# Decoder layer: the first two tiles become the first and second halves of two sequences

## The chip, the cores and the metric

The kernel runs on one core of a Trainium2 chip, in one launch. Its metric is the device time in microseconds (us), the median of several runs. Engines: PE is TensorE, DVE VectorE, ACT ScalarE, POOL GpSimd, SP the engine whose queue starts most DMAs. PEld is TensorE's loading of weights.

## What is computed

Sixteen sequences of 128 tokens with 256 features go through one decoder layer, in float32:

```python
scores = einsum('bhqd,bhkd->bhqk', q, k) / sqrt(16)       # 16 heads, q, k, v from x
scores = where(causal, -inf, scores)
vals, idx = top_k(scores, 32)                             # only the 32 largest keys of a query count
attn = softmax(scores at idx, -inf elsewhere)
x = layernorm(x + (attn @ v) @ Wo.T + bo)
o = relu(x @ proj_in[e].T) @ proj_out[e].T                # for each of 8 experts e
x = layernorm(x + sum over e of gate[e] * o)              # gate[e]: sum of a token's weights whose id is e
xq = quantize(x @ H, 4 bits);  x = layernorm(x + xq @ ternary(weight).T)
```

## The kernel before, in words

The sequences are cut into tiles of 1, 1, 2, 2, 2, 2, 2, 2, 2 sequences (SIZES, line 35). A tile's attention is done in units: one unit is eight heads (one of two halves c of the features) of one sequence, so 32 units. A query of a block of 32 queries sees at most 32, 64, 96 or 128 keys; BLOCKS lists the eight blocks of a unit (two groups of four heads by four query blocks), PLACE their columns in a row of 640 scores.

For each unit: `queries_keys` (264) projects q and k for a feature half of a tile and lays q out in block-diagonal form in `qblk` (for later tiles with eight small DMAs, for the first with multiplications by a mask), `attn_scores` (327) makes four score matmuls, copies them to SBUF on ACT and adds the causal mask on POOL; unit 0 gets its mask by two bf16 matmuls instead. `attn_weights` (357) is the top-k on DVE: four rounds of MAX8 (the eight largest) and MATCH_REPLACE8 (marks them as taken), on blocks with more than 32 keys; blocks with 32 keys take one MAX8 for the softmax's maximum. ACT makes the exponentials. `attn_finish` (405) sums, keeps the taken keys and divides; the division is mostly on POOL. `attn_turn` (421) transposes the weights on PE into `pta` and `ptb` and ACT copies them to `pT`; `attn_apply` (439) multiplies by the values. `attn_end` (450) ends a tile: `py` is the output projection, then residual and norm on DVE, and the transposed result `x1T` (466, through `px`) is what the experts read. `experts` (507) makes for each of eight experts two double halves `ph` (line 551), their relu on ACT, and `po` (521), which ACT scales with the gate and POOL adds up. `token_gates` (481) makes the gates, `ffn` (624) is the last part, run piecewise among the next tile's experts.

The order on PE, DVE, ACT and POOL is that in which the program writes the instructions. A unit has nine steps (STEPS); `plan` says at which step of the running unit other work is written: scores of the next unit at step 1, projections six units ahead, `values` and `residual` (`carry`), the turn of a unit, the end of a tile. `pace` spreads the experts of tile t evenly over the steps between `begin[t]` and `begin[t + 1]`. LAG sets `attn_finish` one step later for units that are not the last of a tile. SP's queue holds the loads, the `qblk` DMAs and the experts' weights (1 MB each), which are written after the projections of (tile 2, half 0) and (tile 3, half 0); the weights of experts 0 to 2 come with the first, of 3 to 7 with the second. Buffers: `xT`, `x`, gate inputs three deep, so a fourth tile's x waits for the first tile's last read of its own.

Of the kernel before, what the change touches and what calls it, by code (L numbers as in the profile page):

```python
# [17 lines left out]
P = 128  # L18
# [11 lines left out]
def decoder_kernel(ctx: ExitStack, tc: tile.TileContext, i: dict, out: bass.AP):  # L30
# [3 lines left out]
    E, DFF = 8, 512  # L34
    SIZES = (1, 1, 2, 2, 2, 2, 2, 2, 2)
    FIRST = [sum(SIZES[:t]) for t in range(len(SIZES))]
# [4 lines left out]
    FIRST_UNITS = DC * SIZES[0]  # L41
# [38 lines left out]

    def load_x(t):
        x = b3.tile([P, TB, D], F32, tag="x", name=f"x{t}")
        nc.sync.dma_start(x[:, : SIZES[t]], i["x"][tokens(t), :].rearrange("(b p) d -> p b d", p=P))
        return x
# [4 lines left out]
    def load_gates(t):  # L89
        n, bs = SIZES[t], slice(FIRST[t], FIRST[t] + SIZES[t])  # L90
        w = b3.tile([P, TB, S], F32, tag="ctx", name=f"ctx{t}")
        nc.sync.dma_start(w[:, :n], i["ctx_512"][bs].rearrange("b k s -> k b s"))
        k = b3.tile([P, TB, S], I32, tag="tok", name=f"tok{t}")
        nc.sync.dma_start(k[:, :n], i["itok"][bs].rearrange("b k s -> k b s"))
        return w, k
# [10 lines left out]
    xT0 = load_T(0, nc.sync)  # L106
# [7 lines left out]
    loaded = xT0, load_x(0)  # L114
    for w, name in ((wqT, "WqT"), (wkT, "WkT")):
        nc.sync.dma_start(w[:, :, ts(1, P)], i[name].rearrange("(c p) o -> p c o", p=P)[:, :, ts(1, P)])
    wvT = weight("WvT", [(nc.sync, slice(0, D))])
    next_loaded = load(1, nc.sync)
# [66 lines left out]
    mask16 = [b1.tile([P, TB, D], BF16, tag=tag, name=f"mask_{tag}").rearrange("p b d -> p (b d)") for tag in ("qi", "qiT")]  # L185
    nc.vector.memset(mask16[0], 0.0)
    nc.vector.memset(mask16[1][:, :P], 0.0)
    for z in (kTs[0], kTs[1], qblks[0][:, 1], odd(vms[0])):
        nc.vector.memset(z, 0.0)
    nc.vector.tensor_reduce(cmask, cm4.rearrange("p h k -> p k h"), AX.X, ALU.add)  # L190

    for k, at, step, count, width in ((0, 320, 128, 2, 2), (0, 96, 128, 2, 1), (1, 32, 64, 2, 1)):
        nc.gpsimd.tensor_copy(
            view(mask16[k], at, [[step, count], [32, width], [1, 32]]),
            cmask.unsqueeze(1).unsqueeze(1).to_broadcast([P, count, width, 32]),
        )
    nc.vector.memset(pTs[0], 0.0)
    for kT in kTs[2:4]:
        nc.gpsimd.memset(kT, 0.0)
    for z in (odd(vms[1]), qblks[1], qblks[2], qblks[3], kTs[4]):  # L200
        nc.gpsimd.memset(z, 0.0)
# [10 lines left out]
    PLACE = {(0, 3): 0, (1, 3): 128, (0, 2): 256, (0, 0): 352, (1, 2): 384, (1, 0): 480, (0, 1): 512, (1, 1): 576}  # L212
    BLOCKS = [(0, 0), (1, 0), (0, 1), (1, 1), (0, 2), (1, 2), (0, 3), (1, 3)]

    def keys(m):
        g, j = BLOCKS[m]
        return slice(PLACE[g, j], PLACE[g, j] + 32 * (j + 1))

# [45 lines left out]
    def queries_keys(t, c, xT):  # L264
# [5 lines left out]
        for j, w in enumerate((wqT, wkT)):  # L270
            for cc in range(DC):
                nc.tensor.matmul(  # L272
                    pps[j][:, j, : n * S], w[:, cc, ts(c, P)], xT[:, cc, : n * S], start=cc == 0, stop=cc == DC - 1
                )
        kT = kTs[(t * DC + c) % len(kTs)]
        qblk = qblks[t] if n == 1 else qblks[(t * DC + c + 2) % len(qblks)]
        if n == 1:
            qblk = qblk[:, c : c + 1]
        ins = None
        if (t, c) == (0, 0):  # L280
            for h in range(HG):
                nc.vector.tensor_scalar(
                    qblk[:, 0, :, h], pps[0][:, 0, :S].rearrange("p (m q) -> p m q", q=32),
                    bq[:, c : c + 1], hmask[:, h : h + 1], ALU.add, ALU.mult,
                )
        else:
            qT = b2.tile([P, TB, S], F32, tag="qT", name=f"qT{t}_{c}")
            ins = nc.scalar.activation(
                qT[:, :n], pps[0][:, 0, : n * S].rearrange("p (b s) -> p b s", b=n), AF.Identity, bias=bq[:, c : c + 1]
            )  # L290
        for g in range(2):
            rows = ts(g, 64)
            ins = nc.scalar.activation(
                kT[rows, :n, g], pps[1][rows, 1, : n * S].rearrange("p (b s) -> p b s", b=n), AF.Identity,
                bias=bk[rows, c : c + 1],
            )
        if (t, c) == (0, 1):
            for h in range(HG):
                src = qT[:, 0].rearrange("p (m q) -> p m q", q=32)
                if h % 2:  # L300
                    nc.scalar.activation(qblk[:, 0, :, h], src, AF.Copy, scale=hmask[:, h : h + 1])  # L301
                else:
                    ins = nc.gpsimd.tensor_scalar(qblk[:, 0, :, h], src, hmask[:, h : h + 1], None, ALU.mult)  # L303
        elif (t, c) != (0, 0):
            for h in range(HC):
                ins = nc.sync.dma_start(
                    qblk[ts(h, DH), :n, :, h % HG].rearrange("p b m q -> p (b m) q"),
                    qT[ts(h, DH), :n].rearrange("p b (m q) -> p (b m) q", q=32),
# [3 lines left out]
    def values(t, xT, x):  # L312
        for b in range(SIZES[t]):
# [13 lines left out]
    def attn_scores(n, qblk, kT, b):  # L327

        parts = [psum(f"ps{k}_{n}") for k in range(2)]
        if n == 0:  # L330

            for k, cols in enumerate((slice(0, 512), slice(512, ROW))):
                part = parts[k][:, : cols.stop - cols.start]
                nc.tensor.matmul(part, ident16, mask16[k][:, : cols.stop - cols.start], start=True, stop=False)
        for j in (3, 2, 1, 0):
# [3 lines left out]
                qblk[:, b, j].rearrange("p h q -> p (h q)"), kT[:, b, :, : 32 * (j + 1)], start=n > 0, stop=n > 0 or j < 2,  # L339
            )  # L340
        if n == 0:

            return lambda m: parts[keys(m).start // 512][:, keys(m).start % 512 :][:, : keys(m).stop - keys(m).start], ins
        sc = b2.tile([P, ROW], F32, tag="sc", name=f"sc{n}")
# [8 lines left out]
        return lambda m: sc[:, keys(m)], ins  # L353
# [3 lines left out]
    def attn_weights(n, sc):  # L357
# [3 lines left out]
        weights[n] = wk  # L361

        nc.gpsimd.memset(wk[:, keys(1)], 0.0)  # L363
        m8 = b2.tile([P, len(BLOCKS), TOPK], F32, tag="m8", name=f"m8{n}")
        nb = b2.tile([P, len(BLOCKS)], F32, tag="nb", name=f"nb{n}")
        z = b2.tile([P, len(BLOCKS)], F32, tag="z", name=f"z{n}")
        d8 = b2.tile([P, len(BLOCKS) - 2, TOPK], F32, tag="d8", name=f"d8{n}")

        def exponentials(ms):

            for m in ms:
                nc.scalar.activation(  # L372
                    ex[:, keys(m)], sc(m), AF.Exp, bias=nb[:, m : m + 1], scale=SCALE,
                    accum_out=z[:, m : m + 1] if m < 2 else None,
# [3 lines left out]
        for r in range(TOPK // 8):  # L378
            left = (lambda m: wk[:, keys(m)]) if r else sc
            for m in range(0 if r == 0 else 2, len(BLOCKS)):  # L380
                nc.vector.max(m8[:, m, ts(r, 8)], left(m))  # L381
            if r == 0:
                nc.vector.tensor_scalar(nb, m8[:, :, 0], -SCALE, None, ALU.mult)
            if r == TOPK // 8 - 1:

                (nc.gpsimd if 3 < n <= LAST[2] else nc.vector).tensor_tensor(
                    d8, m8[:, 2:], m8[:, 2:, 0:1].to_broadcast([P, len(BLOCKS) - 2, TOPK]), ALU.subtract
# [3 lines left out]
            if r == 1 + late:  # L391
                exponentials(range(4))
            if r == 2:
                exponentials(range(4, len(BLOCKS)))
            for m in range(2, len(BLOCKS)):
                nc.vector.match_replace(wk[:, keys(m)], m8[:, m, ts(r, 8)], left(m), TAKEN)  # L396
            yield
        unfinished[n] = wk, ex, z, d8
# [6 lines left out]
    def attn_finish(n):  # L405

        wk, ex, z, d8 = unfinished.pop(n)
        nc.vector.tensor_reduce(z[:, 2:], d8, AX.X, ALU.add)
        rz = b2.tile([P, len(BLOCKS)], F32, tag="rz", name=f"rz{n}")
        nc.vector.reciprocal(rz, z)  # L410
        for cols in (slice(0, PLACE[0, 0]), slice(PLACE[1, 2], ROW)):
# [532 lines left out]
```

## Time and profile before

| | |
|---|---|
| median of 3 runs | 644.65 us (643.78 to 645.05) |
| the profiled execution | 642.72 us, its span 641.0 us |
| busy share of the span | PE 95%, PEld 81%, DVE 78%, ACT 54%, POOL 47% |
| granted TensorE clock, mean | 0.985 |
| experts: ph (line 551) and po (521) | 240.8 and 238.4 us of PE |
| replaces (396) and maxima (381), all forms | MATCH_REPLACE8 132.1 + 42.7, MAX8 100.4 + 38.3 us of DVE |
| first experts' matmul of tiles 0, 1, 2 | 46.49, 88.73, 137.5 us |
| first maxima (start) of the units 0 to 7 on DVE | 8.77, 20.97, 33.54, 50.96, 63.38, 78.42, 92.23, 103.14 us |
| weights of experts 0 and 1 issued on SP | 31.90 to 33.60 us |

A slice of the busy rows is a fortieth of the span, each digit tenths. In a row of the trace, "x8" counts instructions, the mean is in ns, and what stands behind "idle before" or "<-" is what ended the engine's wait. Instructions overlap a little, so a group's time from start to start is shorter than its busy time.

### The profile page before, as it was taken

The page shows a single profiled execution, that of the slowest core. Times are in us where ns is not written, and L with a number is a line of the kernel's source. Part 1 is how long each engine was busy: PE and PEld are TensorE (multiplying, and loading weights), DVE is VectorE, ACT ScalarE, POOL GpSimd, SP SyncE. Part 2 cuts the span into 40 slices and gives each one's busy share as a digit, 9 for nine tenths or more (in the row PEclk, how much of TensorE's full clock was granted, in tenths as well). Part 3 has the DMA queues.
Part 4 walks back from the last instruction along what each step waited for, and adds up shares of the span by engine and source line. Part 5 has one row for each costly group of instructions (what it writes and reads, how often), then busy time and mean ns, then how long its engine had stood idle before and what let it go on. Part 6 is the DMA issues. An engine that isn't in the chain of part 4 may idle for free.

```text
span 641.0 us, 12490 instructions
## 1 busy us (share of the span) xinstructions
PE 605.9 (95%) x3534; PEld 521.9 (81%) x3534; DVE 503.1 (78%) x3133; ACT 346.5 (54%) x1030; POOL 303.5 (47%) x574
## 2 busy tenths in 40 slices
PE   6579999989999999999999999999999999999993
PEld 5468888878888888888888888888888888888882
DVE  7989799799956995789957898579978997332256
ACT  4746666755556565546655655655555655432121
POOL 7114455423753367424772457434673458324322
PEclk9969999999999999999999999999999999999997
DMA  6176700010001000010000000000000000000000
GB/s 205 17 222 214 235 3 10 18 41 2 10 18 38 21 4 16 8 42 2 10 17 19 25 1 10 1 25 2 1 2 0 18 2 2 1 21 0 1 2 33
DMA packets 37990, 21.13 MB, mean 33 GB/s; under 512 B 19104, under 2 KB 35872, under 8 KB 37920
## 3 DMA queue, kind: packets, MB, share of 16 engines
q1 hardware_dynamic: 37360, 20.20, 10.8%
q8 instruction: 28, 0.46, 0.3%
q14 instruction: 42, 0.34, 0.2%
q10 hardware_dynamic: 560, 0.13, 0.1%
HBM read 16.26 MB, written 2.10 MB: 29 GB/s over the span
## 4 chain that ended last, share of the span: by engine, by line
PE 77%; DVE 11%; ACT 5%; POOL 2%; issue 2%; DMA 1%; SPq 1%; ACTq 0%; DVEq 0%; POOLq 0%
PE ph L551 30%; PE po L521 29%; PE ps L337 4%; PE pqk L272 3%; DVE wk L396 3%; PE ptb L445 2%; PE py L457 2%; PE pta L427 2%; DVE m L381 2%; POOL wk L416 2%; PE pv L316 1%; DVE junk L500 1%; ACT ex L372 1%; DVE wk L412 1%; ACT pT L437 1%
## 5 line engine op out<-in xcount | busy, mean ns | idle before, releaser
L551 PE MATMUL ph<-x1T,w_in 128*128 128x256 f32 (+1 forms) x1152 | 240.8, 358 | 0.7 <-ACT hT L555 0.6
L521 PE MATMUL po<-w_out,hT 128*128 128x256 f32 x1024 | 238.4, 381 | 0.0
L551 PEld LDWEIGHTS ph<-x1T,w_in 128*128 128x128 f32 x1152 | 198.7, 190 | 26.5 <-issue 3.4
L521 PEld LDWEIGHTS po<-w_out,hT 128*128 128x128 f32 x1024 | 189.6, 190 | 24.5 <-issue 1.4
L555 ACT ACTIVATE hT<-ph 128x512 f32<-128x512 f32 (+1 forms) x144 | 78.9, 549 | 133.7 <-PE ph L551 133.2
L396 DVE MATCH_REPLACE8 wk<-m,wk 128x64 f32<-128x64 f32 (+2 forms) x576 | 132.1, 239 | 0.0
L529 ACT ACTIVATE part<-po,gate 128x256 f32<-128x256 f32 x112 | 52.9, 472 | 93.2 <-PE po L521 92.5
L381 DVE MAX8 m<-wk 128x8 f32<-128x64 f32 (+2 forms) x576 | 100.4, 241 | 0.0
L416 POOL TENSOR_TENSOR wk<-wk,rz 128x128 f32<-128x128 f32 (+2 forms) x92 | 47.4, 540 | 92.9 <-DVE wk L412 92.9
L532 POOL TENSOR_TENSOR acc<-acc,part 128x512 f32<-128x512 f32 (+1 forms) x56 | 64.4, 1149 | 46.5 <-ACT part L529 45.8
L372 ACT ACTIVATE ex<-sc,nb 128x32 f32<-128x32 f32 (+1 forms) x248 | 74.2, 350 | 0.0
L636 POOL TENSOR_TENSOR xh<-xh 128x256 f32<-128x256 f32 x98 | 67.6, 711 | 1.2
L352 POOL TENSOR_TENSOR sc<-sc,cmask 128x64 f32<-128x64 f32 (+1 forms) x93 | 32.2, 373 | 56.7 <-ACT sc L346 56.7
L337 PEld LDWEIGHTS ps<-kT,qblk 128*128 128x128 f32 x256 | 41.1, 192 | 5.4 <-POOL qblk L303 1.4
L396 DVE MATCH_VALUE_LOAD wk<-m,wk 128x8 f32 x576 | 44.5, 77 | 0.0
L337 PE MATMUL ps<-kT,qblk 128*128 128x256 f32 (+3 forms) x256 | 42.9, 311 | 1.3 <-ACT qblk L301 1.0
L500 DVE SCALAR_TENSOR_TENSOR junk<-wt 128x128 f32<-128x128 f32 x128 | 43.2, 365 | 0.2
L396 DVE MATCH_REPLACE8 wk<-m,sc 128x64 f32<-128x64 f32 (+1 forms) x186 | 42.7, 241 | 0.0
L437 ACT COPY pT<-pta 96x256 f32<-96x256 f32 (+2 forms) x96 | 35.2, 366 | 6.9 <-PE pta L427 6.1
L381 DVE MAX8 m<-sc 128x8 f32<-128x32 f32 (+1 forms) x248 | 38.3, 225 | 0.0
L639 DVE TENSOR_REDUCE qs<-xh 128x2 f32<-128x512 f32 x7 | 4.8, 685 | 36.0 <-POOL xh L636 36.0
L427 PE MATMUL pta<-ident,wk 128*128 128x128 f32 x128 | 20.2, 281 | 12.6 <-POOL wk L363 8.9
(177 smaller groups left out, 667.0 us busy)
## 6 DMA issues: line engine op xcount, KB each, us to landing
w_in<-in_w_in SPq DMA_DIRECT2D x8, 512.0 KB, 6.2
w_out<-in_w_out SPq DMA_DIRECT2D x8, 512.0 KB, 7.1
xT<-in_xT SPq DMA_DIRECT2D x7, 256.0 KB, 3.6
x<-in_x SPq DMA_DIRECT2D x7, 256.0 KB, 2.7
qblk<-qT SPq DMA_DIRECT2D x112, 16.0 KB, 1.9
out_y<-y SPq DMA_DIRECT2D x7, 256.0 KB, 2.1
ctx<-in_ctx SPq DMA_DIRECT2D x7, 128.0 KB, 2.2
tok<-in_itok SPq DMA_DIRECT2D x7, 128.0 KB, 2.2
```

Source lines behind the costliest of these rows:

```text
L337: ins = nc.tensor.matmul(view(parts[PLACE[0, j] // 512], at, [[step, 2], [1, 32 * (j + 1)]]), qblk[:, b, j].rearrange("p h q -> p (h q)"), ...
L372: nc.scalar.activation(ex[:, keys(m)], sc(m), AF.Exp, bias=nb[:, m : m + 1], scale=SCALE, accum_out=z[:, m : m + 1] if m < 2 else None,)
L381: nc.vector.max(m8[:, m, ts(r, 8)], left(m))
L396: nc.vector.match_replace(wk[:, keys(m)], m8[:, m, ts(r, 8)], left(m), TAKEN)
L416: eng.tensor_tensor(view(wk, at, [[step, 2], [1, size]]), view(src, at, [[step, 2], [1, size]]), rz[:, 2 * j : 2 * j + 2].unsqueeze(2).to_ ...
L500: nc.vector.scalar_tensor_tensor(junk, wt[:, 1, b], float(e), wt[:, 0, b], ALU.is_equal, ALU.mult, accum_out=gate[:, b, e : e + 1],)
L521: nc.tensor.matmul(po, hT[:, f, ts(b, S)], w_out[:, e, f], start=f == 0, stop=f == FC - 1)
L529: nc.scalar.activation(part[:, b], po, AF.Copy, scale=gates[t][:, b, e : e + 1])
L532: sums.append(lambda: nc.gpsimd.tensor_tensor(acc[:, :n], (acc if e else x1)[:, :n], part[:, :n], ALU.add))
L551: nc.tensor.matmul(ph[:, f, : n * S], w_in[:, e, c, ts(2 * k + f, P)], x1T[:, c, : n * S], start=c == 0, stop=c == DC - 1,)
L555: ins = nc.scalar.activation(hT[:, ts(k, 2), : n * S], ph[:, :, : n * S], AF.Relu)
L636: nc.gpsimd.tensor_tensor(pairs(xh, c, half), pairs(from_, 0, half), pairs(from_, 1, half), op)
```

## The change

The first two tiles no longer hold one sequence each. Tile 0 is the first 64 tokens of sequences 0 and 1, tile 1 their last 64 tokens; both still have 128 tokens. A query in tile 0 sees at most 64 keys. Units (SUBS, 34 in all):

- tile 0: two EARLY units, each eight heads of both first halves, four blocks of 64 keys with top-k and four of 32 keys. The score is not copied: it stays in PSUM, with its mask by a bf16 matmul of 384 columns.
- tile 1: four LATE units, each eight heads of one sequence's second half, two blocks of 96 and two of 128 keys.

Tile 0 now needs the values of both sequences (made together), and one `xT` buffer, `kT` and `qblk` are shared by the halves. `xT` and `x` of the first two tiles are loaded in more, smaller DMAs, and tile 1's result is stored in two. The projections (1, 0), (1, 1), (2, 0), (2, 1) move to steps 3, 12, 21 and 30; before, (1, 0), (1, 1), (2, 0), (2, 1), (3, 0) stood at 3, 5, 7, 12 and 21. Tile 2's values move from step 7 to 23, tile 3's into the general plan. Experts' weights 0 to 2 now follow projection (1, 1), 3 to 7 follow (2, 0). The subtraction for d moves from POOL to DVE in tile 2's four units, the preparation of the last weights from steps 38 to 56 to 60 to 78, and `begin[1]` from 14 to 10 steps after its last unit.

```diff
+    SUBS = (1, 2, 2, 2, 2, 2, 2, 2, 2)
+    HALF = S // 2
...
+    def load_half(xT, t):
+
+        src = i["xT"][:, : 2 * S].rearrange("(c p) (b h s) -> h c p b s", p=P, b=2, h=2)
+        for c in range(DC):
+            nc.sync.dma_start(view(xT[:, c], t * HALF, [[S, 2], [1, HALF]]), src[t, c])
...
+    EARLY = [(2 * P + 32 * k, 32) for k in range(4)] + [(HALF * k, HALF) for k in range(4)], 4, [(0, 2 * P)], [(4, 4), (0, 4)]
+    LATE = [(256, 96), (352, 96), (0, P), (P, P)], 0, [(0, 448)], [(2, 2), (0, 2)]
...
-        if (t, c) == (0, 1):
+        if (t, c) in ((0, 1), (1, 0)):
...
+        if t == 0:
+
+            part = psum(f"ps_{n}")
+            nc.tensor.matmul(part[:, : 3 * P], ident16, mask16, start=True, stop=False)
+            for b in range(2):
+                for j, at, step in ((1, P * b, HALF), (0, 2 * P + HALF * b, 32)):
+                    ins = nc.tensor.matmul(
+                        view(part, at, [[step, 2], [1, 32 * (j + 1)]]), block(b, j),
+                        kT[:, b, :, : 32 * (j + 1)], start=False, stop=b == 1 and j == 0,
+                    )
+            return part, ins
...
-                (nc.gpsimd if 3 < n <= LAST[2] else nc.vector).tensor_tensor(
-                    d8, m8[:, 2:], m8[:, 2:, 0:1].to_broadcast([P, len(BLOCKS) - 2, TOPK]), ALU.subtract
+                nc.vector.tensor_tensor(
+                    d8, m8[:, short:], m8[:, short:, 0:1].to_broadcast([P, count - short, TOPK]), ALU.subtract
...
-            eng = nc.vector if n < FIRST_UNITS and j > 1 else nc.gpsimd
...
+            (nc.vector if n == 1 and m else nc.gpsimd).tensor_tensor(
...
-        if (t, c) in ((2, 0), (3, 0)):
+        if (t, c) in ((1, 1), (2, 0)):
...
-    lag = {u: LAG for u in range(len(units)) if u > FIRST_UNITS and u not in LAST}
+    lag = {u: LAG for u in range(len(units)) if u not in (LAST[0], *LAST[1:])}
...
-            for k in (2, 3, 4, 4) if quick else (4, 6, 8, 9):
+            for k in ((2, 3, 4, 4), (4, 5, 6, 6), (4, 6, 8, 9))[min(t, 2)]:
...
-    for step, u in ((3, 2), (5, 3), (7, 4), (STEPS + 3, 6), (2 * STEPS + 3, 8)):
+    for step, u in ((3, 2), (STEPS + 3, 4), (2 * STEPS + 3, 6), (3 * STEPS + 3, 8)):
         at(step, project, u)
-    for step, t in ((3, 1), (7, 2), (2 * STEPS + 5, 3)):
+    for step, t in ((2 * STEPS + 5, 2),):
...
-    for step in (38, 40, 47, 49, 56):
+    for step in (60, 62, 69, 71, 78):
...
-    begin = [STEPS * (LAST[t] + 1) + (5, 14)[t] if t < 2 else STEPS * (LAST[t] + 1) + 10 for t in range(NT)]
+    begin = [STEPS * (LAST[t] + 1) + (5, 10, 10)[min(t, 2)] for t in range(NT)]
```

## The prediction

> **What bounds the kernel now.** I first read the busy line of the page, then the busy time by stage, then who waited for whom on TensorE and VectorE up to 145 us, then the two engines in order of time. The slices show where TensorE is not full:
>
> ```profile
> PE   6579999989999999999999999999999999999993
> ...
> DVE  7989799799956995789957898579978997332256
> ...
> PEclk9969999999999999999999999999999999999997
> ```
>
> One slice is 16 us. TensorE is full from the ninth slice to the last but one; VectorE is full in the first nine or so. The stages (expert work of tile 0 begins at 46.49, of tile 1 at 88.73, of tile 2 at 137.5) give the sums; the columns are window and length, then busy us of PE, PEld, DVE, ACT, POOL, then clock and DMA:
>
> ```profile
> 0.00:46.50 46.50, 29.83 (x165) 23.89 (x166) 40.27 (x260) 25.91 (x84) 15.32 (x44) 0.89 0.52 153
> 46.50:88.70 42.20, 39.77 (x300) 35.37 (x298) 38.11 (x256) 27.75 (x95) 22.12 (x48) 1.00 0.53 172
> 88.70:137.50 48.80, 46.13 (x336) 41.01 (x332) 43.27 (x301) 31.07 (x101) 18.41 (x41) 1.00 0.10 23
> 137.50:624.00 486.50, 483.88 (x2706) 417.36 (x2704) 369.87 (x2281) 257.88 (x740) 244.46 (x434) 1.00 0.04 11
> ```
>
> From 137.5 to 624 TensorE misses 2.6 of 486.5 us: there the end is set by the amount of its work. What can change is ahead of it: 16.7 us of idle TensorE before 46.5, 2.4 and 2.7 us in the next two stages, and the half clock in the third slice. The waits of TensorE, and those of VectorE, in that part:
>
> ```profile
> PE pta L427 <- POOL wk L363: 8.9, 4, 5.7
> PE ptb L445 <- ACT pT L437: 4.4, 3, 2.1
> PE pqk L272 <- DMA WqT<-in_WqT: 3.9, 1, 3.9
> PE pta L427 <- POOL wk L416: 2.4, 2, 1.3
> ```
> ```profile
> DVE z L408 <- ACT d L389: 4.2, 3, 3.2
> DVE var_a L239 <- ACT rstd_a L232: 3.0, 1, 3.0
> ```
>
> TensorE's main wait is the transpose pta for the weights of a unit, that is for VectorE (top-k by MAX8 and MATCH_REPLACE8, then GpSimd's multiply). VectorE's own waits are for ScalarE's exponential of d and for rstd; ScalarE works in order and stands behind evictions of TensorE. The last place where TensorE is held is 140.70:
>
> ```profile
> 138.33 0.40 DVE wk L412
> 138.80 1.85 POOL wk L416 x4
> 140.70 0.66 PE pta L427 x4
> ```
>
> So the question is when the first unit of tile 3 has its weights; after that the same work follows in both kernels.
>
> **The parts and their cost.** *Top-k work.* A whole unit makes 26 MAX8 over 2368 columns and 24 replaces over 2304. Two tiles of two units: 104 over 9472 and 96 over 9216. Changed: an early unit makes 20 over 1152 and 16 over 1024, a late one 16 over 1792 and 16 over 1792; two and four of them are again 104 over 9472 and 96 over 9216. Nothing is saved on VectorE, it is re-ordered. The timeline gives start to start: MAX8 at 64 columns 0.13, at 96 0.16, at 128 0.20; load plus replace 0.195, 0.23, 0.26. An early unit is then 0.95 (first maxima) + 0.1 + 0.78 + 3 x 1.30 + 0.3 (d) = 6.0, and 0.75 to finish; a late one 0.75 + 0.1 + 0.98 + 3 x 1.69 + 0.3 = 7.2, and 0.95. The first whole unit ran from 8.77 to 20.97, 12.2.
>
> *TensorE work.* Scores: 640 columns for each of four units before; 2 x 384 + 4 x 448 after, the same 2560, and about 0.2 for the second mask matmul. Transposes 20 before, 22 after, 0.11 each. Values by weights: 64 records of 128 columns (0.57 for 16) become 128 of 64 columns, between half the time each and the same, so from nothing to 2.3 us more in all; I take 0.4 for 16, near the middle, 0.9. It lies mostly in gaps of the head, and only the four late units' share is in the sum below. The projections of tile 2's second half and of tile 3 and tile 3's values leave the head: 1.85 + 1.85 + 1.75 = 5.4 us, to be done among the experts of tile 0.
>
> *Head, walked in order.* The first loads: xT comes as two DMAs of 256-byte runs ahead of WkT, one more issue of 0.5 (SP rows 0.44 to 0.47). "DMA: Bandwidth & Descriptors", section Specifications, in the Trainium skill says transfers below 512 bytes do not reach line rate; by that the 1.3 us by which 128 KB (3.2) land later than a 16 KB qblk load (1.9) could double, +1.3. But those qblk loads have 128-byte runs and land soonest of all, so by the row nothing but the issue. I take +0.4 for the first scores, and get it back from 384 instead of 640 columns: VectorE starts at 8.4 (8.77). Unit 0 to 14.4; unit 1's first round 1.85 and finish of unit 0 0.75: 17.0; its other rounds 4.2: 21.3. Then a new wait: the exponential of d stands on ScalarE behind score copy 0.5, four exponentials 1.1, six pT copies 1.7, qT and kT 1.0, four exponentials 1.0, oT 0.3 (rows of 0.25 to 0.37 each), 5.9 with its own 0.3, from 17.2 on, so it ends at 23.1. Finish 1.1: 24.3. Then pta 0.33, six pT copies 1.7, av 0.6, oT 0.35, py 0.87: 28.2 (py ended at 39.7). To px 2.7 (3.3 before, with six MAX8 between, now four): 30.9. px, scores, two values 2.8: the experts begin at 33.7 instead of 46.5, 12.8 earlier.
>
> *Weights of the experts.* On SP's queue eight qblk DMAs stand ahead of them (0.64 each from about 20.9, to 26), then expert 0, then tile 3's x, which waits for the residual read of tile 0 (28.7), then experts 1 and 2. At the 330 GB/s of 56 to 64 us expert 1 is in at about 34; wanted at 35.5. Cost nothing; if this cover of 1.5 is gone, it is up to 1.5 us.
>
> *Experts of tile 0.* To the exponential of d of the last late unit (unit 5) TensorE has 12 halves of ph at 0.93 (mean of this stage), 5 po at 1.73, scores 2.7, transposes 1.3, av 1.2, projections 3.7, values 1.75: 30.5 to 31, that is 64.5. VectorE has only 30 there (norm 1.9, gates 2.9, three units and a half) and is ahead: it ends unit 5's rounds at 60.9 and waits 3.6 for d, which stands on ScalarE behind po's eviction and oT of unit 4. This is where the early start is given back. Finish 0.95: tile 2 begins on VectorE at 65.6. Before, at 63.4.
>
> *Tile 2.* Before: 63.38, 78.42, 92.23, 103.14, end of tile 118.59. The first gap has the 3.0 wait for rstd, behind qT, kT and a po eviction; in the new order rstd comes ahead of qT, and I expect 0.9. The subtraction of d (POOL, four times) goes to VectorE: 0.3 each. So 65.6 + (15.04 - 3.0 + 0.9 + 0.3) = 78.8; + 13.8 + 0.3 = 92.9; + 10.9 + 0.3 = 104.1; the last: rounds done at 115.3, wait for d 0.5 instead of 3.2 (TensorE has 2 ph and 1 po less in front of it), finish 1.2: 117.3, against 118.6. TensorE reaches the transpose of this unit at 119.3 by its work, the weights are there at 119.5: both tie (120.27 before). Up to py it then has one ph less: py ends at 126.5 (128.2). From there VectorE's chain to the weights of tile 3's first unit is as before: 140.7 becomes 139.1.
>
> **Sum.** 1.6 us earlier: span 641.0 to 639.4, 642.72 to 641.1 by the profiled execution. The median of the runs is 1.9 above that execution; I carry the difference to the median: 643.0.
>
> **Rivals.** *A, given back (0.50):* the above, 641.5 to 644.3. *B, the clock drops in the new gaps (0.26, slower).* TensorE's work around unit 1's end is thinner than before: between 21.4 and 26.4 it has one set of transposes, 0.33 us. Before, the idle time of 5.68 us ahead of 33.8 was followed by clock 0.50 until about 41, and gaps of 2.1 were not. "TensorE: Matmul & The Clock Gate" in the Trainium skill, Part 1 (the HAM clock gate), puts the drop at one whole idle window of some 3.4 us; my longest gap is 2.9, so by the rule it stays warm, by the row 2.9 lies between. If a nearly empty window counts as idle, av 0.6, py 0.87, px, scores and values 2.8 take twice as long, and the projection of 1.85 outlasts the norm by 1.0: 4.5 to 5.2 on the path to 33.7, all of which reaches 64.5. Then 1.6 - 4.5 = 2.9 slower, 647.5. It decides the sign from 1.6 us of added time on. *C, the start is kept (0.14):* if d does not hold VectorE and TensorE waits no more than before, 12.8 - 5.4 = 7.4 earlier, 637.3; half of it, 640, if d at unit 1 and unit 5 come 3 us sooner. Against it: VectorE's work up to tile 3 is equal and it is full in both. *D, slips of 1 to 2 us (0.10):* late weights or in-order waits of ScalarE, 644.3 to 646, no change or a little slower.
>
> About 0.2%, 1.3 us, is what a measurement of this kernel can tell from no change. Below 643.4: 0.36 of A and C, 0.50. Between: 0.13 of A and most of D, 0.22. Above 645.9: B and a rest of D, 0.28. The range goes from the middle of C to B: 639.5 to 647.6.
>
> **What would show it.** Experts of tile 0 begin near 33.7, and TensorE's idle time ahead of them is near 12 instead of 16.7. Clock row: no 0.5 window between 24 and 40 (B: there is one). VectorE waits for d about 2 us near 21 and 3 to 4 us near 61, and starts tile 2 near 65.6, later than before. The rstd wait of 3.0 is gone. The last held pta is near 139. It would be wrong if ph of expert 1 waits for a DMA, if tile 2 starts before 62 (C), or if TensorE loses more than 3 us between 34 and 64.

## The result, and the profile after

The changed kernel takes 650.46 us (649.65 to 651.01, four runs) against 644.64 on the same chip: a ratio of 1.0095, 95% interval 1.0079 to 1.0112. It is 5.8 us slower, where 1.6 us faster was forecast; 650.46 lies above the range as well. Its profiled execution took 650.10 us (span 648.4), that of before 642.72 (span 641.0), so the two traces differ by 7.4; the trace of before is of an execution below all four timed ones.

The slices of the page, one 16.2 us:

```profile
PE   7599988889999999999999999999999999999993
...
DVE  6699799889957898679958799569978998332256
...
PEclk9799999998999999999999999999999999999996
```

TensorE's third slice is full (7 before), so the experts do begin earlier, but the sixth to ninth slice have an 8, and nothing ends earlier. The reason is in VectorE's row. Its stretch from the first maxima to the residual of tile 1 (`r`, line 460 before, 551 after), and from there to the first maxima of tile 3, for the kernel before (columns: window, length, busy us of DVE, then clock and DMA):

```profile
8.77:71.85 63.08, 60.34 (x410) 0.92 0.59 187
71.85:118.59 46.74, 40.07 (x277) 1.00 0.12 30
```

and for the changed kernel:

```profile
9.39:78.87 69.48, 58.99 (x408) 0.93 0.55 173
78.87:124.19 45.32, 42.20 (x287) 1.00 0.12 30
```

In the first stretch VectorE has about the same work in both (60.3 and 59.0), but it was idle for 2.7 us before and is for 10.5 now. With a start 0.6 later, tile 1's `r` comes 7.0 later (78.87 against 71.85). The second stretch is 1.4 shorter. What VectorE waited for in the first stretch, before (us in total, times, longest; the wait for `ps` is that ahead of the first maxima and not in the stretch):

```profile
DVE m L381 <- PE ps L337: 2.3, 1, 2.3
DVE r L460 <- PE py L457: 1.1, 1, 1.1
DVE z L408 <- ACT d L389: 1.0, 2, 0.6
```

and after:

```profile
DVE z L467 <- ACT d L448: 7.7, 4, 3.9
DVE m L440 <- PE ps L372: 3.2, 1, 3.2
DVE r L551 <- PE py L548: 1.9, 1, 1.9
```

So up to tile 1's `r` VectorE was the full engine, and 2.7 us was all that an earlier start of the experts could have taken from it there. The change put 7.8 us of waiting into its queue. Behind `r` there was more idle time to win, 6.7 us of the second stretch before and 3.1 after; but VectorE also has 2.1 us more work there.

**Where these waits come from.** In the head, TensorE has two new holes (timeline of the changed kernel; start, length, and in brackets the idle time ahead):

```profile
19.13 1.02 PE L381 MATMUL ps<-kT,qblk 128*128 128x256 f32 x4 [2.97 <-POOL qblk L331]
...
27.22 0.75 PE L489 MATMUL pta<-ident,wk 128*128 128x128 f32 x3 [2.75 <-DVE wk L476]
...
30.45 2.08 PE L548 MATMUL py<-WoT,oT 128*128 128x256 f32 x4
```

The first is POOL's four masked copies of q for tile 1. ScalarE's copy of the scores behind it stands ahead of all that leads to unit 1's d, but ScalarE itself was busy until 19.66, and waited only 0.53 us for them:

```profile
14.25 0.37 ACT L350 COPY vm<-pv 128x256 f32<-128x256 f32 x1 [0.96 <-PE pv L349]
...
18.02 0.33 ACT L448 ACTIVATE d<-d 128x128 f32<-128x128 f32 x1
18.21 1.06 ACT L227 COPY pT<-zero 128x1024 f32<-128x1024 f32 x1
19.15 0.52 ACT L227 COPY vm<-zero 128x128 f32<-128x128 f32 x2
20.19 0.53 ACT L385 COPY sc<-ps 128x448 f32<-128x448 f32 x1 [0.53 <-PE ps L381]
```

Its list was late from the start: unit 0's exponentials stand behind the copy of tile 0's values, which TensorE, at half speed until about 14 us, delivered at 14.2. In e16 below, with the head's two repairs and full speed from 4.95 on, the same copy of scores begins at 17.16, with the masked copies as ever.

After each hole the clock is at half (window, length, TensorE's busy us, clock):

```profile
20.00:22.00 2.00, 2.00 (x12) 0.64 0.00 0
22.00:24.00 2.00, 1.61 (x34) 0.51 0.43 127
...
28.00:30.00 2.00, 0.98 (x27) 0.50 0.08 12
30.00:32.00 2.00, 2.00 (x20) 0.50 0.57 149
```

`py` took 2.08 us; at the full clock the same four rows take 1.24 to 1.29 (e1, e8). VectorE waits for it 1.9. In the stage of tile 0's experts the picture is that of the forecast. ScalarE just ahead of unit 5's d:

```profile
68.50 0.47 ACT L620 ACTIVATE part<-po,gate 128x256 f32<-128x256 f32 x1 [1.40 <-PE po L612]
68.87 0.68 ACT L431 ACTIVATE ex<-sc,nb 128x128 f32<-128x128 f32 x2
69.46 0.30 ACT L539 ACTIVATE oT<-ptb,bv 128x64 f32<-128x64 f32 x1
69.65 0.30 ACT L448 ACTIVATE d<-d 128x128 f32<-128x128 f32 x1
```

VectorE asked for that d at 66.1 and got it at 69.98, 3.87 later. Last, ahead of tile 3's first weights TensorE waits once more, and drops its clock again:

```profile
146.47 0.82 PE L508 MATMUL pta<-ident,wk 128*128 128x128 f32 x4 [2.70 <-POOL wk L476]
```

That window (148 to 152 us) has a clock of 0.72; before, this wait was 1.28 and the clock 1.00. From this transpose to the end of the execution it takes 503.6 us, before 502.0 from 140.70. In e3's trace the same hole (2.79 us) left the clock at 1.00, and from its transpose, at 149.36, to the end it takes 502.0 as well: so these 1.6 us are the clock's.

### The profile page after: what moved, and what is told of

The parts are those of the page before. It is cut to its first block, busy times and chain, and to the rows that moved or that the text cites. A ratio compares the mean times of both kernels' runs of the same rounds, so it can differ in the third digit from the quotient of the medians.

```text
span 648.4 us, 12632 instructions
## 1 busy us (share of the span) xinstructions
PE 612.3 (94%) x3600; PEld 527.2 (81%) x3600; DVE 504.3 (78%) x3139; ACT 346.7 (53%) x1032; POOL 303.7 (47%) x569
## 4 chain that ended last, share of the span: by engine, by line
PE 81%; DVE 11%; ACT 4%; POOL 2%; issue 1%; DMA 1%; SPq 0%; ACTq 0%; DVEq 0%; POOLq 0%
PE ph L642 32%; PE po L612 29%; PE pqk L296 4%; PE ps L393 4%; DVE wk L455 3%; PE ptb L533 3%; DVE m L440 2%; PE pv L349 2%; PE py L548 2%; PE pta L508 2%; POOL wk L476 1%; DVE junk L591 1%; ACT ex L431 1%; DVE wk L472 1%; DMA WkT<-in_WkT 1%
## 5 line engine op out<-in xcount | busy, mean ns | idle before, releaser
L642 PE MATMUL ph<-x1T,w_in 128*128 128x256 f32 (+1 forms) x1152 | 243.5, 360 | 0.1
L476 POOL TENSOR_TENSOR wk<-wk,rz 128x192 f32<-128x192 f32 (+2 forms) x93 | 48.2, 543 | 97.0 <-DVE wk L472 97.0
L431 ACT ACTIVATE ex<-sc,nb 128x96 f32<-128x96 f32 (+1 forms) x240 | 72.2, 351 | 0.1
L404 POOL TENSOR_TENSOR sc<-sc,cmask 128x64 f32<-128x64 f32 (+1 forms) x84 | 28.9, 370 | 36.1 <-ACT sc L398 36.1
L455 DVE MATCH_REPLACE8 wk<-m,sc 128x96 f32<-128x96 f32 (+1 forms) x184 | 42.5, 241 | 0.0
L393 PEld LDWEIGHTS ps<-kT,qblk 128*128 128x128 f32 x224 | 35.8, 191 | 2.7 <-PE px L563 0.3
L440 DVE MAX8 m<-sc 128x8 f32<-128x96 f32 (+1 forms) x240 | 37.8, 229 | 0.0
L393 PE MATMUL ps<-kT,qblk 128*128 128x256 f32 (+1 forms) x224 | 36.8, 307 | 0.1
L517 ACT COPY pT<-pta 96x256 f32<-96x256 f32 (+2 forms) x84 | 30.7, 366 | 5.6 <-PE pta L508 5.0
L398 ACT COPY sc<-ps 128x512 f32<-128x512 f32 (+1 forms) x56 | 21.1, 429 | 14.0 <-PE ps L393 13.9
```

Of the source, the lines that this page charges most:

```text
L393: ins = nc.tensor.matmul(view(parts[PLACE[0, j] // 512], at, [[step, 2], [1, 32 * (j + 1)]]), block(b, j), kT[:, b, :, : 32 * (j + 1)], st ...
L431: nc.scalar.activation(ex[:, keys(m)], sc[:, keys(m)], AF.Exp, bias=nb[:, m : m + 1], scale=SCALE, accum_out=z[:, m : m + 1] if m < short ...
L440: nc.vector.max(m8[:, m, ts(r, 8)], left[:, keys(m)])
L476: (nc.vector if n == 1 and m else nc.gpsimd).tensor_tensor(view(wk, at, dims), view(src, at, dims), rz[:, m : m + k].unsqueeze(2).to_broad ...
L642: nc.tensor.matmul(ph[:, f, : n * S], w_in[:, e, c, ts(2 * k + f, P)], x1T[:, c, : n * S], start=c == 0, stop=c == DC - 1,)
```

## The experiments

My theory after the trace: the head is late (holes, half clock, a later WkT), and in the stage behind it d of unit 5 stands behind TensorE's work on ScalarE. The rival: the waits are only symptoms of orders in the queues, each of which can be moved. Each kernel ran beside the kernel before on one chip (643.2 to 644.5 us there), and is compared with that. The edits are to the changed kernel unless said otherwise.

**e1_warm: fill the holes.** Dummy products of the identity; their results are not used.

```diff
+    def warm(n, name):
+        pd = pso.tile([P, 512], F32, tag="po", name=f"warm{name}")
+        for _ in range(n):
+            nc.tensor.matmul(pd[:, :P], ident, ident, start=True, stop=True)
+    for step, n in ((4, 10), (15, 10), (19, 4)):
+        at(step, warm, n, step)
```

> The changed kernel with 24 extra identity matmuls (their result is read by nobody) written into TensorE's three gaps before the experts of tile 0: 10 after the projection (1, 0), 10 after the values product of unit 0, 4 after the transposes of unit 1. If the half clock between 27 and 34 us is a main cause, no such window is left, py takes 1.0 instead of 2.0 us, the experts of tile 0 begin near 35.8 instead of 38.3, and since TensorE's work and then VectorE follow from there, the time falls by 2 to 2.5 us to about 648. If the path to the end does not pass there, the experts begin earlier but the time stays within 0.5 us of 650.5.

649.07 us, ratio 1.0091 (1.0061 to 1.0120). The clock stays at 1.00 from 16 to 56, `py` takes 1.24, the experts begin at 35.34 instead of 38.32. Of these 3.0 us, `r` of tile 1 keeps 2.5 (76.41). Not all of the 3.0 is the dummies': unit 1's scores, ahead of the first of them and with the same instructions up to there, begin at 12.59 here and at 14.21 in the changed kernel, because the half speed at the start ended earlier. In e2, e5, e11 and e14, again the same up to there, they begin at 12.94 to 13.22, and the experts still at 38.00 to 38.30; so most of it is the holes'. The interval alone can't tell this kernel from the changed one; the pairs below, which have e3's edit too, can.

**c1_before_warm: the same in the kernel before**, at steps 15, 16 and 19, where its long hole is.

> The kernel before with 28 extra identity matmuls, read by nobody, in its gap of 5.7 us ahead of the transposes of unit 1 and behind them. No half clock between 33 and 41. By my reading VectorE is what holds until 140 us, and only its wait for py of 1.1 us goes: 643.5. If the clock itself sets the time, the experts begin 2.5 to 3 us earlier and the time falls by as much, to 642.

643.28, ratio 0.9989 (0.9977 to 1.0000). The half clock there, between 34 and 41 us, cost about 0.7 (by the interval between nothing and 1.5): VectorE was nearly full and hid it (`r` waits 0.2 for `py` instead of 1.1).

**e3_loads: WkT's first half on ScalarE's queue**, behind WqT, instead of behind the two xT loads on SP.

```diff
     wqT = weight("WqT", [(nc.scalar, ts(0, P))])
+    wkT = weight("WkT", [(nc.scalar, ts(0, P))])
...
-    wkT = weight("WkT", [(nc.sync, ts(0, P))])
```

> The changed kernel with the first half of WkT loaded from ScalarE's queue, behind WqT, instead of behind the two xT loads on SP. The wait for WkT of 0.6 us goes, the first scores come 0.6 us earlier. If TensorE's slow start (0.4 us a matmul until 14 us, before only until 8.5) follows from that gap, the second projection and the values run at full speed too and unit 2's scores come 2 us earlier (17 instead of 19.1); the time falls by 1.5 to 2.5, to about 648.5. If only the load itself counts: 650.0.

649.73, ratio 1.0100 (1.0075 to 1.0126): alone no gain that the runs tell apart. The wait for WkT is gone, VectorE starts 0.9 earlier, the experts begin at 37.02 and `r` comes at 78.09. The holes and the half clock stay; in this trace, its slowest execution, the tiles behind `r` take the rest back.

**e4_warm_loads: both repairs.**

> The changed kernel with both head repairs: the idle gaps of TensorE at 16 and 25 us filled with dummy matmuls of the identity (their products are not used), and the first half of WkT loaded from ScalarE's queue behind WqT. If the head's two costs (the clock that fell in the gaps, the later WkT) are separate and both last to the end, the gains add: experts of tile 0 at 34 us, 648.0 us in all. If the stage after the head gives back what starts earlier, the second repair adds nothing to the first: 649 us, although the experts begin at 34.

647.50, ratio 1.0065 (1.0048 to 1.0081). The two holes have shrunk:

```profile
PE pta L489 <- DVE wk L476: 0.8, 1, 0.8
PE ps L381 <- POOL qblk L331: 0.7, 1, 0.7
```

Experts at 35.09, `r` at 76.16. Measured beside e5 on the same chip, whose own edit moved nothing, it is 2.7 us faster; the pairs e12 and e11, e15 and e14 below give 2.7 and 2.6. So the head's holes and loads are worth 2.6 to 2.7 us. The three kernels without the repairs are 6.5 to 7.4 us slower than the kernel before on their chips, those with them 3.9 to 4.8.

**e10_split: the masked copies on two engines.** `if h % 2 and t == 0:` becomes `if h % 2:`, so ScalarE makes two of the four.

> The changed kernel with two of the four masked copies of q of tile 1 (first channel half) on ScalarE, as tile 0 has them, instead of all four on GpSimd. TensorE's wait for them (3.0 us at 16 us) should shrink to about 1.8 us, and the clock stay up there. If that gap matters: experts at 36.5 us, total 648.5 to 649.5. If ScalarE's two added copies delay unit 0's or unit 1's exponentials instead: 650.5 or more.

650.52, ratio 1.0092 (1.0074 to 1.0109). Nothing gained: the first hole is 1.9 instead of 3.0, a second of 1.6 follows at unit 0's weights, the one ahead of unit 1's transposes is 2.4, and the clock between 24 and 32 us is still 0.50.

**e2_pace: tile 0's experts spread over ten more steps.** `begin[1]` is 20 instead of 10 steps behind tile 1's last unit.

> The changed kernel with begin[1] 20 instead of 10 steps after tile 1's last unit, so that the experts of tile 0 are spread over 51 steps instead of 41. If the wait of VectorE for the exponential of d of unit 5 (3.9 us, because ScalarE stands behind TensorE's experts) is what gives the early start back, that wait shrinks below 1.5, tile 2 starts on VectorE 2.5 to 3.5 us earlier (near 68), TensorE's waits between 80 and 128 shrink, and the time falls to about 647.5. If the end is set by the amount of TensorE's work left, later experts cannot help: 650.5 or more.

653.40, ratio 1.0158 (1.0125 to 1.0190), a miss: slower instead of faster. The stage from the first experts to `r`, in this kernel (window, length, busy us of PE, PEld, DVE, ACT, POOL, clock, DMA):

```profile
38.08:78.70 40.62, 36.18 (x272) 31.39 (x271) 35.12 (x237) 23.02 (x74) 14.35 (x30) 0.96 0.53 171
```

and in the changed kernel:

```profile
38.32:78.87 40.55, 39.05 (x309) 34.81 (x308) 35.68 (x237) 23.44 (x73) 15.55 (x32) 1.00 0.55 180
```

TensorE has 2.9 us less to do there and the stage is as long as before. That does not clear TensorE, though. What was put off left a hole of 1.95 us ahead of unit 2's transposes, and the projections behind it ran at half clock (1.92 and 1.86 us, 1.03 each in the changed kernel):

```profile
44.54 0.70 PE L503 MATMUL pta<-ident,wk 128*96 128x128 f32 x4 [1.95 <-POOL wk L476]
45.03 1.92 PE L296 MATMUL pqk<-xT,WqT 128*128 128x256 f32 x4
46.74 1.86 PE L296 MATMUL pqk<-xT,WkT 128*128 128x256 f32 x4
```

From those transposes to 71.17 TensorE is busy for 26.35 of 26.63 us; in the changed kernel, from the same transposes at 44.38 to 70.90, for 26.37 of 26.52. Later the work that was put off is missed: the last d of tile 2 waits 5.2 us, and holes up to 3.7 us bring the clock to 0.87 between 78.7 and 130.

**e5_lag5: unit 5 is closed one step later**, behind the first maxima and replaces of unit 6.

```diff
-        if n not in lag:
+        if n not in lag and n not in soon:
...
+    soon = {LAST[1]: 1}
...
-        if u in lag:
-            at(s + lag[u], attn_finish, u)
+        if u in lag or u in soon:
+            at(s + {**lag, **soon}[u], attn_finish, u)
```

> The changed kernel with one edit: the closing of unit 5 (the sum that needs the exponential d, reciprocal, is_equal multiply) is issued on VectorE one step later, behind the first MAX8 and the first replaces of unit 6, so that VectorE has work of tile 2 while ScalarE is late with d. Theory (the 3.9 us at unit 5's d is VectorE standing still behind an in-order ScalarE, and VectorE's chain sets the end): tile 2's first MAX8 at about 67 instead of 70.9 us, the end 3 to 3.9 us earlier, 646.5 to 647.5 us. Rival (TensorE is what is behind there, VectorE only meets it): the time comes back as a later wait for a later d or for the scores of units 7 to 9, and the total stays at 650.

650.20, ratio 1.0103 (1.0083 to 1.0123): the rival's number. Tile 2 starts on VectorE at 66.24, 4.7 earlier, but then `r` waits 2.7 for `py` and 1.2 of the wait for d is left; unit 7's first maxima begin at 83.75 (83.67 in the changed kernel).

**e6_lasts and c2_before_lasts: the last unit of every tile but the last is closed later**, in e6 with both head repairs (`soon = {LAST[0]: 0, **{u: 1 for u in LAST[1:-1]}}`), in c2 in the kernel before, from tile 1 on.

> The changed kernel with the two head repairs and with the closing of the last unit of every tile but the last moved behind work of the next tile (unit 1: behind the first MAX8 of unit 2; units 5, 9, 13 and on: behind the first MAX8 and replaces of the next tile). If VectorE's waits for d are what the change lost and each is only an order in VectorE's queue, this is 643 to 645 us, level with the kernel before. If TensorE and ScalarE are the later ones by tile 2, it is 647 to 649.

> The kernel before with the closing of the last unit of tiles 1 to 7 moved one step later in the same way. It waited 3.2 us for a d at 118 us and 3.0 for an rstd; if the order of VectorE's queue is all of that, 641 to 642 us; if the other engines are the later ones at that place, no change: 644.

651.93 (ratio 1.0133, 1.0114 to 1.0151) and 651.59 (1.0128, 1.0110 to 1.0146): 4.4 us slower than e4 and 8 slower than the kernel before; both expectations missed. Each tile's end comes a step later, and `r` waits for `py` (in c2 2.8 at tile 1, 3.2 at tile 2); I did not follow what it costs in the later tiles. Moved in this way, the waits for a tile's last d are not time that can be won.

**e7, e8, e9: projections back into the head.** In e7 (2, 0), (2, 1) and tile 2's values stand where the kernel before has them, (1, 1) at step 5; in e8 they are put into the holes; e9 is e8 with WkT moved and dummies in the first hole. The first new line is e7's (values at step 7), the second that of e8 and e9 (values at 19).

```diff
-    for step, u in ((3, 2), (STEPS + 3, 4), (2 * STEPS + 3, 6), (3 * STEPS + 3, 8)):
+    for step, u in ((3, 2), (5, 4), (7, 6), (STEPS + 3, 8)):
+    for step, u in ((3, 2), (STEPS + 3, 4), (15, 6), (23, 8)):
```

> The changed kernel with one part of the change undone: the projections of tile 1's second channel half and of tile 2, and tile 2's values, are emitted in the head at the steps where the kernel before has its own (5, 7, 12; values at 7). Theory (the projections that the change moved out of the head, about 5 us of TensorE, make TensorE and so ScalarE late in the stage of tile 0's experts; in the head they lay in idle gaps): d of unit 5 waits 0 to 1 us instead of 3.9, tile 2 starts on VectorE near 67 us, the total is 646 to 648. Rival (in front of the head's chain the same work delays tile 0's end, and ScalarE's copies stand ahead of the exponentials): experts of tile 0 start 3 us later, near 41 us, and the total is 650 to 652.

> The changed kernel with tile 2's projections and values moved into TensorE's idle gaps of the head (its first channel half behind unit 1's d, so in the gap at 25 us, the values into the gap ahead of py, the second half into the one ahead of px). They then cost nothing where they stand, keep the clock up at 25 us, and take about 4 us out of the stage of the experts. If that stage is TensorE's, d of unit 5 waits under 1 us and the total is 645.5 to 647.5. If what sets tile 2's start is not TensorE's load in that stage but the time at which the experts begin, only the clock's share is gained: 648.5 to 650.

> The same, with WkT's first half on ScalarE's queue and dummy products of the identity in the remaining gap at 16 us: all repairs of the head that I know of together. By the theory (head's clock, WkT, and projections, each worth 1 to 2 us) 643 to 645 us, level with the kernel before. By the rival (stage A' ends no earlier) 647 to 648 us, as with the head repairs alone.

651.31 (ratio 1.0110, 1.0088 to 1.0133), 649.41 (1.0078, 1.0058 to 1.0097) and 648.80 (1.0074, 1.0052 to 1.0097). Only (2, 1) really left the stage by this, the other projections were in the head already, which I had overlooked. e7 is the rival's number: later head. In e8 the stage from experts to `r` is 39.7 instead of 40.6, and `py` of tile 0 has its full clock; but px now waits 3.1 us behind the norm, and the experts begin at 38.38, no earlier. The wait at unit 5's d is 3.9 in all three.

**e11 and e12: tile 3's first projection and values later** (e12 with both repairs).

```diff
-        at(STEPS * u + 5, project, u + 6)
+        at(STEPS * u + (19 if u == 4 else 5), project, u + 6)
...
-            at(STEPS * u + 7, carry, units[u + 6][0])
+            at(STEPS * u + (21 if u == 4 else 7), carry, units[u + 6][0])
```

> The changed kernel with tile 3's first projection and its values emitted 14 steps later, in tile 2's units, where TensorE had some 7 us of idle time between 72 and 120 us. If TensorE's load in the stage from 36 to 70 us is why d of unit 5 comes late, about 4 us of TensorE leave the stage: the wait falls from 3.9 to under 1 us, tile 2 starts on VectorE at 67 to 68 us, the total is 646.5 to 648. If the order in ScalarE's queue or the pace by steps is the cause, the wait stays above 3 us and the total at 650.

> The same with the head's two repairs (dummy products of the identity in the gaps, WkT's first half on ScalarE's queue), which alone made 647.5 with the wait for unit 5's d still at 3.9. If head and stage are the two separate costs, the gains add up: 643.5 to 645, level with the kernel before. If one of them is a shadow of the other: 646.5 to 647.5.

651.05 (ratio 1.0112, 1.0091 to 1.0132) and 648.39 (1.0066, 1.0043 to 1.0089). These did not test what they should: unit 5's plan asks for the same projection at step 50, so that it landed right ahead of d on ScalarE, and only the values moved. The wait at d is 3.7, now with this reason.

**e14 and e15: the projection really at step 55**, by `STEPS * u + {4: 19, 5: 10}.get(u, 5)`; e15 with both repairs.

> As e11, but the projection now really stands at step 55, behind unit 5's d. In e11's trace ScalarE was free for d at 66.65 us and VectorE asked for it at 66.2. If TensorE's load in the stage is the cause: wait under 1 us, tile 2's first MAX8 at 67.5, and the end 3 us earlier, 647 to 648. If what is gained there comes back in tile 2 (the moved work meets tile 1's end, r waiting for py, units 6 and 7 waiting for their scores): wait gone, total still 650.

> The same with the head's two repairs, which alone made 647.5. If the two costs are separate and both last, 644 to 645 us, level with the kernel before. If tile 2 gives back what the stage gains: 647 to 648.5.

650.77 and 648.17 (ratios 1.0115, 1.0101 to 1.0129, and 1.0073, 1.0059 to 1.0087). VectorE's two longest waits from 40 to 86 us in e14:

```profile
DVE r L551 <- PE py L548: 2.7, 1, 2.7
DVE z L467 <- ACT d L448: 1.3, 1, 1.3
```

The wait at d is gone but for 1.3: TensorE's projection and values ahead of it were the cause of the other 2.6. Tile 2 starts at 67.87 in e14, and at 65.6 in e15. But `r` then waits 2.7 for `py`, because the moved work, at steps 55 and 57, still stands ahead of `py` (step 58). Put behind it, it was not tried.

**e13_all_as_before: every projection where the kernel before has it**, tile 3's first at step 21.

> The changed kernel with the whole order of projections and values undone: tile 1's second half, tile 2's and tile 3's first are all in the head again, at the steps of the kernel before. Theory: the wait at unit 5's d goes (under 1 us), but the head's chain has the work in front of it, experts of tile 0 begin near 41 us, total 647 to 650. Rival (the order of projections is not what costs): wait 3.9 as ever, total 651.

677.77, and no evidence: tile 3's q falls into the buffer from which unit 3 still has to read tile 1's, so unit 3's scores are of another q, and VectorE waits 26.5 us for them.

**e16_start_warm: e4 with eight dummy products of a zero tile ahead of the first projection.**

```diff
     def attention():
+        pd, cold = pso.tile([P, 512], F32, tag="po", name="warm0"), kTs[1][:, :, 0, :HALF]
+        for _ in range(8):
+            nc.tensor.matmul(pd[:HALF, :P], cold[:, 0], cold, start=True, stop=True)
         project(0)
```

> The changed kernel with the head's two repairs (dummy products in the gaps, WkT's first half on ScalarE's queue; 647.5 us), and eight dummy products of a zero tile ahead of the first projection, from about 2 us on, while TensorE waits for WqT (their sums are not used). If the half speed at the start hangs on how late TensorE's work begins: full speed by 8 instead of 12 us, first MAX8 at 8.0 to 8.3 instead of 8.6, experts of tile 0 at 33.5 to 34 instead of 35.1, total 646 to 646.7. If it hangs on the idle time inside the start (the 0.6 us that TensorE waits ahead of the first scores), half speed lasts to 11 us or more as before and the total stays at 647.5.

647.28, ratio 1.0055 (1.0041 to 1.0068), not told apart from e4. The head did get shorter: full speed by 5 us, experts at 34.41, `r` at 75.47. It came back at tile 2's last d, which waits 3.7 here and 2.6 in e4. That goes with the clock: some 20 us ahead of it TensorE waits as long in both, but in e16 (the first row) the four transposes and what follows run slower than in e4 (clock 0.51 from 100 to 102 us, in e4 1.00):

```profile
99.67 0.81 PE L508 MATMUL pta<-ident,wk 128*128 128x128 f32 x4 [2.17 <-DVE wk L455]
```
```profile
100.36 0.66 PE L508 MATMUL pta<-ident,wk 128*128 128x128 f32 x4 [2.16 <-DVE wk L455]
```

**All runs together.** From the profiled executions, in us:

| kernel | experts begin | tile 1's `r` | between | execution minus `r` |
|---|---|---|---|---|
| before | 46.49 | 71.85 | 25.4 | 570.9 |
| c1 (before, dummies) | 48.78 | 72.37 | 23.6 | 571.1 |
| changed | 38.32 | 78.87 | 40.6 | 571.2 |
| e1 | 35.34 | 76.41 | 41.1 | 571.6 |
| e4 | 35.09 | 76.16 | 41.1 | 571.3 |
| e5 | 38.00 | 78.57 | 40.6 | 572.4 |
| e8 | 38.38 | 78.07 | 39.7 | 572.0 |
| e14 | 38.30 | 78.61 | 40.3 | 572.6 |
| e15 | 35.94 | 76.35 | 40.4 | 572.5 |
| e16 | 34.41 | 75.47 | 41.1 | 571.9 |
| e2 (pace) | 38.08 | 78.70 | 40.6 | 577.4 |
| c2, e6 (tiles closed later) | 48.06, 35.66 | 75.77, 76.22 | 27.7, 40.6 | 575.3, 575.1 |

(e7, e9 to e12 lie within these: between 39.7 and 41.1, last column 571.5 to 572.3. e3's profiled execution was its slowest, 573.3.) Two facts follow. Where the later tiles are left alone, the time is tile 1's `r` plus 570.9 to 572.6, in both kernels. In part these sums agree by chance: in the changed kernel the second stretch is 1.4 us shorter and the end, by the last drop of the clock, 1.6 longer. And from the first experts to that `r` the changed kernel takes 39.7 to 41.1, whatever I moved inside. So the head counts nearly one to one; what I moved inside the stage came back at `py` (e5, e14, e15) or, in e8 and e9, won at most 0.9.

No kernel here beats the kernel before by more than its interval; c1 is level with it.

## Why the prediction was wrong

Forecast for the profiled execution were 641.1 us, measured 650.10. Of these 9.0 us the head makes 4.6, the stage of the experts 0.7, tile 2 2.1 and the end 1.6. The step that failed first is the head's: it put nothing for the longer half speed at the start and nothing for the drop of the clock in the holes. Behind it, tile 2's last d and the assumption of the same end in both kernels failed too.

- **VectorE's work is only re-ordered:** right, 60.3 and 59.0 us up to `r`. So was the consequence that a full VectorE leaves little to gain. "It is full in both" holds up to `r` only: from there to tile 3 it was busy for 40.1 of 46.7 us before.
- **The head: this step failed.** First maxima at 8.4: 9.39. The cost of the smaller loads was put at 0.4, without the wait for WkT (0.6), and the first scores ran at half speed. "d of unit 1 waits 2 us near 21": 0.9 for unit 0 and 2.35 for unit 1, ending at 25.7, because the walk began ScalarE's list at 17.2; it began at 20.19. The half speed at the start, longer than before, is most of that: in e16, without it and with the head's two repairs, the first maxima come at 8.32, the list begins at 17.16 and d ends at 23.2 (forecast 8.4, 17.2, 23.1). "py ends at 28.2": 32.5, at half clock; 28.6 in e16. Experts at 33.7: 38.32; 34.41 in e16. I gave rival B, the drop of the clock in the gaps, 0.26 and priced it at 4.5 to 5.2. In e1, with the holes filled, the experts begin 2.7 to 3.0 earlier than in e5, e11, e14 and the changed kernel, a part of which is the start. B's sign was right; that its price comes near the head's 4.6 is luck, since it left out the start.
- **The stage of the experts:** 30.5 to 31 to unit 5's d was forecast, 31.3 measured; the wait 3.6, measured 3.87. "This is where the early start is given back" was right, and e14 shows that TensorE's projection and values there cause 2.6 of it. What was not seen is that `py` of tile 1 stands close behind: in the changed kernel `r` finds `py` done with 0.5 us to spare (77.13 + 1.26 against 78.87), so the wait could hardly have been won in VectorE's order.
- **Tile 2:** start 65.6, measured 70.91, 5.3 late with the head. rstd's wait is gone, as said. "Wait for d 0.5 instead of 3.2": 2.56, in other traces of these kernels 3.7 (see the last section). Together with 1.8 for rstd at tile 2's end, tile 3's first weights come at 146.47 instead of 139.1.
- **The end:** "after that the same work follows in both" missed the last hole of 2.70 us, after which the clock fell: 1.6 us.

Even with the experts at 33.7 the sign would not have been saved: 33.7 + 40.6 is 74.3 for `r`, and with 571.2 to the end 645.5 against 642.7: what failed behind the head, 0.7, 2.1 and 1.6 us, is more than the 1.6 us of the forecast gain. e16, at 34.41, comes close to this case.

**Open.** The head's repairs give 2.6 to 2.7 us back; 3.9 to 4.8 remain (e4, e12, e15), and 3.8 with full speed from the start (e16). In e4's trace they are there at tile 1's `r`: 76.16 against 71.85. TensorE's queue ahead of `py` is the nearest reason (39.1 of 40.6 us busy in the changed kernel, 23.8 of 25.4 before), and e2 does not speak against it, since the clock took back what the edit spared. But no run took work out of that queue between unit 2's transposes and `py` without a drop of the clock, except for the one projection, (2, 1), of e7 to e9; so it is not shown.

## What to carry to other kernels

Ask first which engine is full up to the place from which the rest follows, and add up its start, its work and its idle time; if its idle time is 2.7 us, an earlier start of another engine can't be worth 12 up to there. Then look for one event whose distance to the end is the same in all kernels, and judge every edit by that event. A wait that goes where you moved an instruction, and reappears at the next dependence on the same engine, was never the cause.

## What was not expected of the hardware

The clock fell after idle times of 2.97, 2.75 and 2.70 us, in e2 after one of 1.95, and in e10 behind holes of 1.9 and 1.6; in e3 one of 2.79 left it at 1.00. The clearest case is a hole of 2.15 to 2.17 us ahead of a transpose in tile 2, which the changed kernel and fourteen of its variants share: in eight of these traces the clock fell behind it, in seven it stayed at 1.00. Where it stayed, VectorE waits 2.56 us for tile 2's last d (in e6 that wait is not there), where it fell, 3.66 to 4.31, and tile 1's `r` is 571.9 to 573.3 from the end instead of 571.2 to 571.9 (e6 aside). All these holes are shorter than the one idle window of some 3.4 us in "TensorE: Matmul & The Clock Gate", Part 1, of the Trainium skill, by which the forecast kept its holes of up to 2.9 us warm; the length of the hole alone does not decide it here.

At the start the profile's clock reads 1.00 (changed kernel, 4 to 16 us) while the matmuls run at half speed. In the changed kernel's trace that lasted until about 14 us, in the one before until about 8.5, in e4 until about 11. In e1, e2 and e7, with the changed kernel's instructions up to there, it was over at 10.4 to 10.9: so where it ends differs from execution to execution. With dummy products from 1.75 us on (e16) it was over at 4.95:

```profile
1.75 3.27 PE L957 MATMUL warm<-kT 128*64 128x128 f32 x16 [1.75 <-DVE kT L209]
4.95 0.71 PE L296 MATMUL pqk<-xT,WqT 128*128 128x128 f32 x4
```

The same four rows of `pqk` take 1.22 us in the changed kernel.
